# Four residual layers on one NeuronCore: where averages, halo copies, loads and banks stand in the issue order

## The chip, the cores and the metric

The kernel runs on one core of a Trainium2 chip as a single launch. Its engines each work through their own instruction queue in order: TensorE (PE in the profile, its weight loads PEld), VectorE (DVE), ScalarE (ACT), GpSimd (POOL) and SyncE (SP, which only issues DMAs). The metric is the device time of the launch in microseconds. The kernel before was timed three times.

## What is computed

The input is 1024 images of 16 x 16 positions and 16 channels in float32. Four layers follow, each of the form x + layer(group norm of x). The norm takes the mean and variance of pairs of channels over an image.

```python
x = x + _L0_conv_ref(_gn(x), core0, core1, core2)     # tensor train
x = x + _L1_conv_ref(_gn(x), ...)                     # cellular automaton
x = x + _L2_conv_ref(_gn(x), filters, bias)           # 3x3 convolution
x = x + _L3_conv_ref(_gn(x), ...)                     # as layer 1

# layers 1 and 3, per image:
p = jnp.concatenate([xt, y1, y2], axis=1)       # y1, y2: Sobel filters
flat = p.reshape(B * W * Hh, 48)
h = jax.nn.relu(flat @ fc0_w.T + fc0_b)         # first dense layer, 128 wide
d = (h @ fc1_w.T + fc1_b).reshape(B, C, W, Hh)  # second dense layer
mask = (pre & post)                             # 3x3 maxima of channel 3
```

Layer 0 is a matrix of 4096 x 4096 in tensor-train form, with ranks 16, applied to each image.

## The kernel before

The batch is cut into two chunks of 512 images, and a chunk fills one of two resident tiles of 32 lines (`XN`, 128 partitions x 512 each line). A chunk is either in the layout "cw" (channels and columns chosen by the line) or "wc". Every engine's order is written out by hand: the program is run as Python, and instructions are issued in the order in which the functions are called (`tc.manual_schedule`). A float32 product leaves two matmul records in the profile; a transpose leaves one.

`run` (L1534) drives each stretch. It takes a list of main steps, the products of a layer, and background lists with costs in microseconds. Each background step gets a due point between 0 and 1 from the costs; bare numbers are pauses. After main step i all background steps that are due are issued, in order. At the last main step everything left is issued.

Layer 0 runs as five phases of 16 units. `build` (L1045) makes a unit's weights in four banks `pw` of the "w" pool from a tile `gq`, which SP loads from `g_dram` (L1040); ScalarE copies them out (L1062). During the first phase (main steps: 64) the background turns the rest of the first chunk by transposes `ptin` (L866), loads the second chunk in eight loads of 1 MB on POOL's queue (`load`, L848), makes further tiles g (`gs`, L581, stored by SP, L563) and turns the second chunk. These transposes and g products take banks by the tag "mw", which alternates between the pools "w" (four banks) and "m" (one bank) by the variable `either` (L144). POOL also stores the turned lines (L881).

Layers 1 and 3 (`layer_nca`, one run for each chunk: four "dense runs" in the text) go by `plan`: a slot is either a set of row tiles of 32 x 128 of the first dense layer (`ph`, L1521, evicted by ScalarE, L1524) or a block of the second dense layer (`po`, L1358, four column tiles of 128 x 32, evicted by VectorE, L1370). Some three to five row slots lie between two dense slots. `po` has two banks, tagged "o", and the averages of the background norm take theirs from the same two (`psum`, with `shared` set to "o").

The background norm of the other chunk is `norm_cw` (L782), by quarters of eight lines, or `norm_lines` (L709). Sums run on VectorE; a mean is a product with an averaging matrix (`pmean`, L749 or L717), the variance likewise (`pvar`, L753 with 32 columns, L721 with 128). ScalarE copies the mean (`held`), VectorE subtracts it; squares run on ScalarE in layer 2 and on VectorE in the dense runs.

Layer 2 (`layer_conv`, L1190) has 54 main steps for a chunk. Each row h has products of three row offsets (`inner`, L1222) in two banks and one contribution across halves (`across`, L1231) that reads a halo tile `hx`. ScalarE fills a halo tile in eight copies (L1210), queued in `pending`, one issued after each main step until the queue is empty. ScalarE also evicts the banks (`finish`, L1270), and POOL adds them to DRAM by DMA. Six banks hold three rows.

The last dense run turns its output for storing: `turn` (L1416) transposes into `ptx`, VectorE copies, and with the last tile SP stores 1 MB pieces to the output. The last four quads are done in two halves of the batch (`hf` 0 and 1), and `after(n, fn)` delays fn by n slots.

Of the kernel before, what the change touches and what calls it, by code (L numbers as in the profile page):

```python
# [19 lines left out]
P = 128  # L20
# [83 lines left out]
def conv_preact_kernel(ctx: ExitStack, tc: tile.TileContext, a: dict, out: bass.AP):  # L104
# [35 lines left out]
    either = [0]  # L140
# [567 lines left out]

    def norm_lines(X, on_act=True):  # L709
# [3 lines left out]
        st = {}  # L713

        def mean():
            st["p"] = psum([P, NB], "pmean")
            T.matmul(st["p"], gm_wc, s1["s"], start=True, stop=True)  # L717

        def var():
            st["v"] = psum([P, NB], "pvar")  # L720
            T.matmul(st["v"], gm_wc, s2["s"], start=True, stop=True)  # L721
# [5 lines left out]
        subs = each(X, 0, NL, lambda: st["m", 0], ALU.subtract)  # L727
        steps = steps + [5, mean, 2, held(st), 2] + centred(subs, more)
# [3 lines left out]
    def parts_cw(X, on_act):  # L732
# [3 lines left out]
        for q in range(4):  # L736
# [10 lines left out]
            def mean_q(s1=s1):  # L747
                st["p"] = psum([P, NB], "pmean")
                T.matmul(st["p"], gm_cw, s1["s"], start=True, stop=True)  # L749
# [17 lines left out]
            N["mean"].append(mean_q)  # L767
            N["var"].append(var_q)
# [13 lines left out]
    def norm_cw(X, on_act):  # L782
# [6 lines left out]
        for q in (1, 2):  # L789
            steps += woven(  # L790
                sums[q + 1], (1, var[q - 1]), (3, keep[q - 1]), (3, mean[q]), (4, hold[q])
            ) + [2] + sq[q][:4]
            if q == 1:
                steps += sq[q][4:]
# [231 lines left out]
    def layer_train():  # L1026
# [18 lines left out]
        def build(u):  # L1045
# [7 lines left out]
            pw = [bank([P, 2, 16 - 4 * k0, S], "w", "pw") for _ in range(4)]  # L1053
            for v in range(2):
# [135 lines left out]
    def layer_conv(X, n, other):  # L1190
# [64 lines left out]
        def step(*fs):  # L1255
            def go():
                for f in fs:
                    f()
                if pending:
                    pending.pop(0)()  # L1260

            return go
# [22 lines left out]
    def layer_nca(X, n, l, L, xo=None):  # L1285
# [119 lines left out]
        def residual(q, w2, hf=None):  # L1405
# [7 lines left out]
            else:  # L1413
                after(8, lambda: turn(q, w2, r, hf))
# [66 lines left out]
        def step(slot):  # L1481
            def go():
# [4 lines left out]
                else:  # L1487
                    for x in slot:
                        tile_of_row(*x)
                due = [fn for n, fn in later if n <= t]  # L1490
# [43 lines left out]
    def run(layer, us, loads, *spans, by=0.0):  # L1534
# [21 lines left out]
        for i, step in enumerate(main):  # L1556
# [5 lines left out]
            while todo and (todo[0][0] < part or i == len(main) - 1):  # L1562
                todo.pop(0)[1]()
# [23 lines left out]
    with ExitStack() as es:  # L1587
# [33 lines left out]
        ]  # L1621
        run(
            steps_of(phases[0]), 130, (),
            (late[:6] + loads[0:4] + late[6:] + loads[4:] + later + woven_in + tail + normed(0, 1) + combined(0, False), 0.0, 1.0),
# [35 lines left out]
    with ExitStack() as es:  # L1660
# [8 lines left out]
            (lambda: None, main1), 108, load_cw(X0, xf[3][0]) + [put(L3)], (norm_cw(X0, True), 0.09, 1.06), by=0.07  # L1669
# [38 lines left out]
```

## Time and profile before

| what | value |
|---|---|
| median of three runs | 3043.31 us (3041.16 to 3043.62) |
| the profiled execution: its time / its span | 3039.35 us / 3037.6 us |
| mean granted TensorE clock | 0.992 |
| layer 0, first phase and what lies ahead of it | 0 to about 192 us |
| layer 0, other phases | about 192 to 1759 us |
| layer 1, two dense runs | about 1760 to 2276 us |
| layer 2, two chunks | about 2277 to 2494 us |
| layer 3, two dense runs | about 2494 to 3020 us |
| last stores | to 3037.6 us |

TensorE is busy 98% of the span, but a busy TensorE isn't one at its peak: the ends of matmuls are modelled, and at half clock it is busy too. So the profile is read by the start times of successive operations in the timeline: 56 records of 128 x 512 of an undisturbed unit take 24.23 us. A bracket behind a line of the timeline gives the idle time before it and the engine whose work ended it.

### The profile page before, as it was taken

The page shows a single profiled execution, that of the slowest core. Times are in us where ns is not written, and L with a number is a line of the kernel's source. Part 1 is how long each engine was busy: PE and PEld are TensorE (multiplying, and loading weights), DVE is VectorE, ACT ScalarE, POOL GpSimd, SP SyncE. Part 2 cuts the span into 40 slices and gives each one's busy share as a digit, 9 for nine tenths or more (in the row PEclk, how much of TensorE's full clock was granted, in tenths as well). Part 3 has the DMA queues.
Part 4 walks back from the last instruction along what each step waited for, and adds up shares of the span by engine and source line. Part 5 has one row for each costly group of instructions (what it writes and reads, how often), then busy time and mean ns, then how long its engine had stood idle before and what let it go on. Part 6 is the DMA issues. An engine that isn't in the chain of part 4 may idle for free.

```text
span 3037.6 us, 36802 instructions
## 1 busy us (share of the span) xinstructions
PE 2973.1 (98%) x13810; PEld 1245.4 (41%) x13810; DVE 1764.0 (58%) x2352; ACT 1102.7 (36%) x1822; POOL 669.9 (22%) x727
## 2 busy tenths in 40 slices
PE   7999999999999999999999999999999999999997
PEld 4444334444444444444444433333333333333333
DVE  5354337555554555544555668756977765856433
ACT  4431441000000000000101156666667656666564
POOL 2135670200000000000000015434542223442321
PEclk9999999999999999999999999999999999999998
DMA  8643664533334333332222235436337866343466
GB/s 313 232 120 99 150 152 145 166 109 109 109 109 158 115 109 109 109 102 89 88 89 94 71 130 168 137 119 204 124 122 182 188 97 207 126 129 111 134 176 208
DMA packets 251522, 418.39 MB, mean 138 GB/s; under 512 B 34869, under 2 KB 105065, under 8 KB 248273
## 3 DMA queue, kind: packets, MB, share of 16 engines
q1 hardware_dynamic: 225776, 362.53, 36.2%
q0 software_dynamic: 25376, 53.38, 8.5%
q8 instruction: 109, 1.79, 0.2%
q14 instruction: 69, 0.56, 0.1%
q10 hardware_dynamic: 192, 0.13, 0.0%
HBM read 238.58 MB, written 165.53 MB: 133 GB/s over the span
## 4 chain that ended last, share of the span: by engine, by line
PE 92%; DVE 2%; DMA 1%; issue 1%; ACT 1%; POOL 1%; SPq 0%; DVEq 0%; POOLq 0%; ACTq 0%
PE po L1134 51%; PE ph L1521 22%; PE po L1358 8%; PE po L1222 4%; PE pw L1057 3%; PE po L1231 1%; PE L_conv_pe L392 1%; PE ptin L866 1%; DVE bn L860 1%; PE ptx L1420 1%; PE pvar L753 1%; PE pr L765 0%; PE pmean L749 0%; POOL res L1410 0%; ACT hx L1210 0%
## 5 line engine op out<-in xcount | busy, mean ns | idle before, releaser
L1134 PE MATMUL po<-xn,w 128*128 128x512 f32 x3584 | 1573.9, 596 | 1.2 <-DVE xn L946 1.1
L1134 PEld LDWEIGHTS po<-xn,w 128*128 128x128 f32 x3584 | 670.3, 190 | 839.8 <-issue 820.6
L1524 ACT ACTIVATE hid<-ph,pack 128x512 f32<-128x512 f32 (+1 forms) x1040 | 656.2, 680 | 381.3 <-PE ph L1521 267.7
L1170 DVE TENSOR_TENSOR r<-r,po 128x512 f32<-128x512 f32 x576 | 377.9, 684 | 577.4 <-PE po L1134 525.0
L1409 POOL TENSOR_TENSOR u<-u,mask 128x512 f32<-128x512 f32 x123 | 192.9, 1568 | 1815.3 <-DVE mask L1403 1395.6
L1062 ACT COPY w<-pw 128x512 f32<-128x512 f32 (+1 forms) x320 | 150.6, 556 | 1209.9 <-issue 1006.3
L1521 PE MATMUL ph<-xn,wq 32*128 32x512 f32 (+1 forms) x3752 | 568.8, 600 | 0.0
L1521 PEld LDWEIGHTS ph<-xn,wq 32*128 32x128 f32 x3752 | 239.4, 184 | 268.2 <-issue 235.9
L1521 PE MATMUL ph<-xn,pack 32*128 32x512 f32 x1288 | 298.6, 624 | 4.9 <-ACT hid L1524 3.0
L1358 PE MATMUL po<-hid,pack 128*32 128x512 f32 (+1 forms) x2080 | 282.1, 602 | 0.0
L1075 DVE TENSOR_TENSOR w<-w 128x512 f32<-128x512 f32 x320 | 210.9, 686 | 88.7 <-ACT w L1062 88.6
L655 DVE TENSOR_TENSOR xn<-xn,m 128x1024 f32<-128x1024 f32 x160 | 216.0, 1380 | 47.2 <-ACT m L678 47.0
L1410 POOL TENSOR_TENSOR res<-res,u 128x512 f32<-128x512 f32 x123 | 205.4, 1670 | 9.7
L1370 DVE SCALAR_TENSOR_TENSOR u<-po,pack,xn 128x512 f32<-128x512 f32 (+1 forms) x130 | 96.3, 741 | 189.9 <-PE po L1358 185.6
L1222 PE MATMUL po<-xn,convw 128*128 128x512 f32 x368 | 167.8, 608 | 2.9 <-ACT conv L1270 2.9
L1521 PEld LDWEIGHTS ph<-xn,pack 32*128 32x128 f32 x1288 | 115.1, 185 | 104.1 <-issue 64.6
L1170 DVE TENSOR_TENSOR xn<-xn,po 128x512 f32<-128x512 f32 x96 | 64.4, 684 | 123.7 <-PE po L1134 123.3
L1358 PEld LDWEIGHTS po<-hid,pack 128*32 128x32 f32 x2080 | 43.6, 108 | 193.0 <-issue 142.3
L622 DVE TENSOR_TENSOR sq<-sq 128x1024 f32<-128x1024 f32 x78 | 109.8, 1408 | 13.3 <-ACT sq L640 12.6
L1222 PEld LDWEIGHTS po<-xn,convw 128*128 128x128 f32 x368 | 69.1, 192 | 100.3 <-issue 91.5
L404 POOL DMA_DIRECT2D L_conv_wy<-xn x160 | 89.1, 565 | 27.5 <-ACT xn L398 16.2
L1057 PE MATMUL pw<-R,gq 32*128 32x256 f32 (+1 forms) x1280 | 88.4, 381 | 3.1 <-DMA gq<-g_dram 2.9
(166 smaller groups left out, 1770.1 us busy)
## 6 DMA issues: line engine op xcount, KB each, us to landing
xf<-r SPq DMA_DIRECT2D x112, 512.0 KB, 3.8
xn<-xf SPq DMA_DIRECT2D x96, 512.0 KB, 5.1
r<-xf SPq DMA_DIRECT2D x80, 512.0 KB, 4.5
wq<-L_conv_wy SPq DMA_DIRECT2D x192, 192.0 KB, 2.7
res<-xf SPq DMA_DIRECT2D x128, 256.0 KB, 3.2
xf<-res SPq DMA_DIRECT2D x96, 256.0 KB, 2.1
res<-xr SPq DMA_DIRECT2D x256, 64.0 KB, 2.8
xf<-conv POOLq DMA_DIRECT2D x64, 256.0 KB, 5.9
```

The costliest lines, as they stand in the source:

```text
L655: V.tensor_tensor(part, part, m().unsqueeze(1).broadcast_to([P, 2, NB]), op)
L1057: T.matmul(pw[r][:, v], st["g", u][rows, v], st["R"][rows, p % 2, 64 * k0 : 256], start=True, stop=True,)
L1062: A.copy(w[:, k0:4, :, 32 * r : 32 * r + 32].rearrange("p k t (v o) -> p v (k t) o", v=2), pw[r],)
L1075: V.tensor_tensor(w[:, k], w[:, x], w[:, y], ALU.add if sign > 0 else ALU.subtract)
L1134: T.matmul(po, st["w", u][:, matrix, t], x, start=t == 0, stop=t == 3)
L1170: V.tensor_tensor(r[at], r[at], po, ALU.add if sign > 0 else ALU.subtract)
L1222: T.matmul(st["po", h][wh], conv["fw"][:, y], X[:, 16 * wh + h + y - 1], start=y == max(0, 1 - h), stop=y == min(2, S - h),)
L1358: T.matmul(po[32 * j : 32 * j + 32], nca["w1"][:, v], hid[j], start=v == 0, stop=v == 1)
L1409: by.tensor_tensor(u, u, st["m"][:, w2, cols(hf)], ALU.mult)
L1410: by.tensor_tensor(r, r, u, ALU.add)
L1521: T.matmul(ph, w, x, start=k == 0, stop=k == len(tiles) - 1)
L1524: A.activation(h, ph, AF.Relu, bias=nca["bt"][:, r : r + 1])
```

## The change

There are seven edits. `average` makes the product with the averaging matrix: as one product where the shared pool is "m", as four column tiles of 32 where it is "o". `beside_dense` marks the means and variances; `run` holds a marked step, and all background steps behind it, until the main step just issued was a block of the second dense layer or the last one. A main step without the attribute `dense` (layers 0 and 2) counts as near. In `norm_cw` the variance of the quarter before stands one sum later. `build` sets `either`, so that the next "mw" bank comes from the pool "m". The halo copies of layer 2 are issued after four of every seven main steps (numbers 2, 4, 6 and 7), not after each. The turn in the last halves is due after four slots, not eight. The eight loads of the second chunk are put between the turns, and between the products of g, one for every two of these. In layer 2 the second chunk's background norm begins at 0.12 of the stretch, not 0.09.

```diff
@@ -706,6 +706,19 @@
 
         return [2, root, 3, (6, newton)]
 
+    def beside_dense(fn):
+
+        fn.beside = True
+        return fn
+
+    def average(out, w, x):
+        if shared[0] == "m":
+            T.matmul(out, w, x, start=True, stop=True)
+            return
+
+        for c in range(0, P, 32):
+            T.matmul(out[c : c + 32], w[:, c : c + 32], x, start=True, stop=True)
+
     def norm_lines(X, on_act=True):
         parts = [lambda l=l: X[:, l : l + 2] for l in range(0, NL, 2)]
         s1, steps = line_sum(parts, "s1", False)
@@ -714,17 +727,18 @@
 
         def mean():
             st["p"] = psum([P, NB], "pmean")
-            T.matmul(st["p"], gm_wc, s1["s"], start=True, stop=True)
+            average(st["p"], gm_wc, s1["s"])
 
         def var():
             st["v"] = psum([P, NB], "pvar")
-            T.matmul(st["v"], gm_wc, s2["s"], start=True, stop=True)
+            average(st["v"], gm_wc, s2["s"])
 
         def keep():
             st["ve"] = work([P, NB], "n", "ve")
             V.tensor_scalar(st["ve"], st["v"], GN_EPS, None, ALU.add)
 
         subs = each(X, 0, NL, lambda: st["m", 0], ALU.subtract)
+        mean, var = beside_dense(mean), beside_dense(var)
         steps = steps + [5, mean, 2, held(st), 2] + centred(subs, more)
         steps += [5, var, 2, keep] + rstd(st)
         return steps + by_rows(each(X, 0, NL, lambda: st["r"], ALU.mult))
@@ -746,7 +760,7 @@
 
             def mean_q(s1=s1):
                 st["p"] = psum([P, NB], "pmean")
-                T.matmul(st["p"], gm_cw, s1["s"], start=True, stop=True)
+                average(st["p"], gm_cw, s1["s"])
 
             def var_q(rows=rows, s2=s2):
                 st["v"] = psum([P, NB], "pvar")
@@ -764,8 +778,8 @@
                 st["p"] = psum([P, NB], "pr")
                 T.matmul(st["p"], sel[rows], st["r"][rows], start=True, stop=True)
 
-            N["mean"].append(mean_q)
-            N["var"].append(var_q)
+            N["mean"].append(beside_dense(mean_q))
+            N["var"].append(beside_dense(var_q))
             N["keep"].append(keep_q)
             N["held"].append(held(st, q))
             N["spread"].append(spread_q)
@@ -788,7 +802,7 @@
         steps = sums[0] + woven(sums[1], (2, mean[0]), (3, hold[0])) + [1] + sq[0]
         for q in (1, 2):
             steps += woven(
-                sums[q + 1], (1, var[q - 1]), (3, keep[q - 1]), (3, mean[q]), (4, hold[q])
+                sums[q + 1], (2, var[q - 1]), (3, keep[q - 1]), (3, mean[q]), (4, hold[q])
             ) + [2] + sq[q][:4]
             if q == 1:
                 steps += sq[q][4:]
@@ -1051,6 +1065,8 @@
 
             k0 = 2 if m1 == 2 else 0
             pw = [bank([P, 2, 16 - 4 * k0, S], "w", "pw") for _ in range(4)]
+
+            either[0] = 1
             for v in range(2):
                 for r in range(4):
                     rows = slice(32 * r, 32 * r + 32)
@@ -1256,7 +1272,9 @@
             def go():
                 for f in fs:
                     f()
-                if pending:
+
+                st["n"] = st.get("n", 0) + 1
+                if pending and st["n"] % 7 % 2 == 0:
                     pending.pop(0)()
 
             return go
@@ -1411,7 +1429,7 @@
             if xo is None:
                 after(7, lambda: nc.sync.dma_start(tile_cw(xf[l + 1][n], 8 * q + w2), r))
             else:
-                after(8, lambda: turn(q, w2, r, hf))
+                after(8 if hf is None else 4, lambda: turn(q, w2, r, hf))
 
         def turn(q, w2, r, hf):
             g0, n = (0, 4) if hf is None else (2 * hf, 2)
@@ -1487,6 +1505,7 @@
                 else:
                     for x in slot:
                         tile_of_row(*x)
+                go.dense = isinstance(slot, int)
                 due = [fn for n, fn in later if n <= t]
                 later[:] = [x for x in later if x[0] > t]
                 for fn in due:
@@ -1560,6 +1579,9 @@
                 loads[done]()
                 done += 1
             while todo and (todo[0][0] < part or i == len(main) - 1):
+                near = getattr(step, "dense", True) or i == len(main) - 1
+                if getattr(todo[0][1], "beside", False) and not near:
+                    break
                 todo.pop(0)[1]()
 
     def put(L):
@@ -1619,9 +1641,15 @@
         woven_in = [
             x for j in range(2) for i in range(4) for x in stat[j][i] + lines[j][4 * i : 4 * i + 4]
         ]
+
+        def mixed_in(xs, ys):
+
+            n = len(xs)
+            return [z for i, x in enumerate(xs) for z in (*ys[2 * i : 2 * i + 2], x)] + ys[2 * n :]
+
         run(
             steps_of(phases[0]), 130, (),
-            (late[:6] + loads[0:4] + late[6:] + loads[4:] + later + woven_in + tail + normed(0, 1) + combined(0, False), 0.0, 1.0),
+            (late[:6] + mixed_in(loads[0:4], late[6:]) + mixed_in(loads[4:], later) + woven_in + tail + normed(0, 1) + combined(0, False), 0.0, 1.0),
         )
         run(
             steps_of(phases[1]), 350, (),
@@ -1666,7 +1694,7 @@
         bg = bg[:-16] + woven(bg[-16:], *[(6 + i, copy) for i, copy in enumerate(first1)])
         run((lambda: now(first0), main0), 108, load_wc(X1, xf[2][1]), (bg, 0.09, 1.04), by=0.07)
         run(
-            (lambda: None, main1), 108, load_cw(X0, xf[3][0]) + [put(L3)], (norm_cw(X0, True), 0.09, 1.06), by=0.07
+            (lambda: None, main1), 108, load_cw(X0, xf[3][0]) + [put(L3)], (norm_cw(X0, True), 0.12, 1.06), by=0.07
         )
     with ExitStack() as es:
         shared[0] = "o"
```

## The prediction

> **What bounds the kernel now.** I read the page first (busy shares, slices, chain of waits), then TensorE's timeline in each stretch the diff touches, then ScalarE, VectorE and the DMA windows there.
>
> ```profile
> PE 2973.1 (98%) x13810; PEld 1245.4 (41%) x13810; DVE 1764.0 (58%) x2352; ACT 1102.7 (36%) x1822; POOL 669.9 (22%) x727
> PE 92%; DVE 2%; DMA 1%; issue 1%; ACT 1%; POOL 1%; SPq 0%; DVEq 0%; POOLq 0%; ACTq 0%
> ```
>
> TensorE carries the chain. From 480 to 1759 us a unit of 56 product records takes 24.23 us with nothing between but its build, and the diff doesn't touch that. What can be won is where TensorE waits, switches its tiling, or runs at a lower clock. TensorE's timeline, layer 0, first phase (start, length, operation, idle before it and its releaser):
>
> ```profile
> 61.91 0.48 PE L1057 MATMUL pw<-R,gq 32*128 32x128 f32 x2
> 63.03 0.48 PE L1057 MATMUL pw<-R,gq 32*128 32x128 f32 x2 [0.65 <-DMA gq<-g_dram]
> 66.24 1.19 PE L1057 MATMUL pw<-R,gq 32*128 32x128 f32 x10 [0.88 <-DMA gq<-g_dram]
> 67.36 1.97 PE L866 MATMUL ptin<-ident,xn 128*128 128x128 f32 x8
> 69.12 3.62 PE L1134 MATMUL po<-xn,w 128*128 128x512 f32 x4
> 72.54 1.09 PE L866 MATMUL ptin<-ident,xn 128*128 128x128 f32 x8
> ...
> 104.39 0.73 PE L1057 MATMUL pw<-R,gq 32*128 32x128 f32 x16
> 105.56 1.09 PE L866 MATMUL ptin<-ident,xn 128*128 128x128 f32 x8 [0.44 <-ACT w L1062]
> ...
> 114.77 0.73 PE L1057 MATMUL pw<-R,gq 32*128 32x128 f32 x16
> 115.43 1.17 PE L866 MATMUL ptin<-ident,xn 128*128 128x128 f32 x8
> ```
>
> The build at 61.91 waits for gq, whose DMA takes 13.22 us in the chain against a median of 2.2: the four 1 MB input loads were issued at 50.37. Then four records take 3.42 us (69.12 to 72.54) where they otherwise take 1.72: half clock. At 104.39 the transposes follow the build after 1.17 us, at 114.77 after 0.66: the former's bank waits for the build's first ScalarE copy.
>
> The convolution (layer 2), TensorE and ScalarE:
>
> ```profile
> 2335.71 7.13 PE L1222 MATMUL po<-xn,convw 128*128 128x512 f32 x16
> 2345.78 5.40 PE L1222 MATMUL po<-xn,convw 128*128 128x512 f32 x8 [2.94 <-ACT conv L1270]
> ...
> 2398.63 1.13 PE L749 MATMUL pmean<-s1s,gm_cw 128*128 128x512 f32 x2 [2.39 <-DVE s1s L630]
> ...
> 2413.05 1.04 PE L753 MATMUL pvar<-s2s,gv_cw 128*32 128x512 f32 x2 [2.67 <-DVE s2s L630]
> 2414.03 3.67 PE L1222 MATMUL po<-xn,convw 128*128 128x512 f32 x4
> ...
> 2345.04 1.27 ACT L1270 ACTIVATE conv<-po,b 128x512 f32<-128x512 f32 x2
> ```
>
> Three stalls, 8.0 us. After the first, eight records take 5.33 us (3.44 at full clock, 1.9 lost); after the third, four take 3.47 (1.75 lost). The second lowers no clock.
>
> The dense layers (layers 1, 3), and the DMA windows at the very end (from the left: stretch, length, five engines, granted clock, DMA share, GB/s):
>
> ```profile
> 1844.67 1.12 PE L749 MATMUL pmean<-s1s,gm_cw 128*128 128x512 f32 x2
> 1845.73 0.70 PE L1521 MATMUL ph<-xn,wq 32*128 32x512 f32 x2
> ...
> 3013.00:3015.00 2.00, 2.00 (x24) 1.11 (x18) 0.38 (x2) 1.17 (x4) 0.00 (x0) 1.00 0.00 0
> 3020.00:3023.00 3.00, 0.00 (x0) 0.00 (x0) 0.50 (x2) 0.00 (x0) 0.00 (x0) 0.79 0.97 404
> ```
>
> A mean takes 1.06 us among row tiles, for 0.86 us of work. At the end the DMAs are idle until the first half's stores start at 3015.27, then move some 420 GB/s to the end: there the stores are the bound.
>
> **What the Trainium skill says.** "TensorE: Matmul & The Clock Gate", What's actually happening: the clock halves after an idle window of about 3.4 us that runs freely. Agrees in kind: 2.67 and 2.94 us of idleness halved it, 2.39 didn't. "TensorEngine Tiling (Array Packing)", Key Properties: changing the tiling mode drains the array; the 0.2 us above is that. "DMA: Bandwidth & Descriptors", Queues, rings and completion order: an engine alternates between rings by whole packets; it fits four small gq transfers taking 13 us beside four large loads. The first page (Architectural detail) calls ScalarE and VectorE strictly first-in first-out; the late eviction at 2345.04, queued behind squares and copies, agrees.
>
> **The change part by part.** Against the profiled execution: span 3037.6 us, 3039.35 with what lies around it. The median of the runs shown, 3043.31, is 3.96 above; I carry the difference over to it.
>
> *Loads one by one.* Only one load, not four, then stands before the gq of 51.43, and the pairs of line stores lie between the loads on POOL. The stretch 61.91 to 72.54 is 10.63 us; at full pace it is 0.66 (build) + 0.87 (8 transposes) + 1.72 (4 records) = 3.25. Gain 7.4. What is late next: POOL waits for no product, and between the second four loads there is no POOL work (the g builds use TensorE, ScalarE, SP), so these four still go back to back, about 71 us in the new order. But two g builds now come right before them, so the 512 KB store of g goes onto SP ahead of m_dram and the gq that the build of unit 5 needs (about 76 issued, needed near 85.5; four loads at some 400 GB/s occupy the DMAs 10 us). Bounds 0 to 4 us; I take 1.3, about half of one to three. Net 6.1. Statistics and turns of the second chunk keep their places, 10 us or more after the loads land.
>
> *Other bank behind builds.* In nine of the builds (at 40.87, 92.39, 104.39, 124.71, 134.65, 144.59, 154.53, 164.46, 174.40) the next work takes a "w" bank and begins 1.17 instead of 0.66 us later: 9 x 0.51 = 4.6. The second turn then gets the "w" bank, 0.43 us later, when the copy is done, as at 115.43. One g pair now follows a build directly: minus 0.5. Net 4.1.
>
> *Averages beside the dense layer.* Eleven means (full array) become four column tiles like those of the second dense layer, and together with eight one-column variances (L753) wait until a dense step has run. A lone mean costs 1.06 plus about 0.2 for closing the row group before it; beside a dense block 0.86. By due times six lie alone (0.4 each), five already next to one (0.2): 3.4. Six of the variances lie alone (0.3 each): 1.8. Cost: an average that isn't let through holds all background work behind it, up to 4 us. VectorE has that slack (73% busy in the first dense run), and the delayed sums remove no cover. But with variance one step later, two pairs (variance of quarter 1 with mean of 2 in the first run; of 0 with mean of 1 in layer 3) fall due at one dense step. The second then needs one of only two "o" banks: it waits for an eviction of VectorE (0.69 us for the variance, behind an addition of 1.22), about 1 us; the first such wait stands there now too (0.97 at 2600.80). Net 5.2 - 1.5 = 3.7; bounds -3 (each wait doubled, some clock) to 7.
>
> *Even copies, layer 2.* The eviction that ends the first stall goes behind seven halo copies since its group began (1.04 us each); now four. But it also stands behind a square whose subtraction VectorE ends at 2342.72; VectorE loses 0.70 to a late square at 2335.82, and that goes. So square done 2343.1, one copy to 2344.15, eviction 0.85 us sooner: stall 2.94 to 2.1. Under the 2.39 that halved nothing, so 1.9 of clock comes back: 2.8. Bounds 0.5 (clock still drops) to 4.8.
>
> *Layer 2, second chunk.* Start 0.12: the first mean falls one step later (1.72 us), its stall 2.39 becomes 0.65. The first variance falls two steps later (3.44): TensorE comes at 2410.37 - 2.39 + 0.65 + 3.44 = 2412.1 for a sum at 2413.05, stall 1.0 instead of 2.67, and the clock (1.75) holds. Sum 5.2. VectorE's chain is the limit afterwards: it gains about 2.6 us from the earlier mean, TensorE 5, so an eviction behind squares is late next, about 1.2. Net 4.0; bounds 1 to 6.8.
>
> *Last halves.* The turn of the first half (ptx at 3014.15) moves four slots forward, to when its sum is ready (3011.93): 1.9 us, with 0.3 for short waits. The stores start that much sooner and fill the DMAs to the end, so the end moves by 1.9; bounds 1 to 2.6.
>
> Sum: 6.1 + 4.1 + 3.7 + 2.8 + 4.0 + 1.9 = 22.6 us. Profiled 3016.8; median 3043.3 - 22.6 = 3020.7.
>
> **The rivals.** (1) Everything clears: 7.4 + 4.6 + 6 + 4.8 + 6.8 + 2.2 = 31.8, 3011.5. For it: each stall has one named releaser. Against: in layer 2 VectorE's chain stands just behind. (2) New waits take the place: gq of unit 5 costs 4 with clock, layer 2 gives 2 in all, the averages nothing: 3.4 + 4.1 + 0 + 2 + 1.9 = 11.4, 3031.9. For it: in-order ScalarE behind VectorE-paced squares. (3) Nothing to measure: the averages lose 10 and layer 2 gives 1, total 0.4 us gained, 3043. For it: only that TensorE is busy 98%. (4) Slower: held averages release background work in bursts, evictions on VectorE come late, and TensorE waits in the dense runs long enough for the clock. The stall of 2.97 us at 1779.94, followed by half clock until about 1785, shows the price: 3 + 2.5 = 5.5 us. The other parts give 18.9, so from five such stalls among the 19 averages it is slower; eight give 44 - 18.9 = 25 lost, 3068. Against: the sum of the dense block's own output is issued to VectorE ahead of the burst.
>
> **How the numbers follow.** Forecast 0.46 (3015 to 3027), (1) 0.24, (2) 0.18, (3) 0.07, (4) 0.05. A measurement tells about 0.2% from no change, 6 us. The first three are faster: 0.88; same 0.07; slower 0.05. Range 3009 to 3033: it takes in (1) and (2) and leaves out (3), (4) and the outer ends.
>
> **What would show it.** Right: no wait for gq near 62 and full clock to 75; 0.66 us behind every build; the stall near 2345 under 2.4 us without half clock; first store of the last halves some 2 us sooner before the end. Wrong: a gq wait near unit 5; a mean waiting over 2 us for VectorE in a dense run; evictions of layer 2 later than now.

## The result

The changed kernel takes 3022.86 us (median of four runs, 3019.86 to 3025.54), the kernel before 3043.47 (four runs, 3041.16 to 3044.03): ratio 0.9933, 95% interval 0.9916 to 0.9951. The forecast was 3020.7. The profiled execution took 3019.86 us with a span of 3018.2, so 19.4 us of span went, against 22.6 in the sum. Line numbers of the changed kernel are some 14 to 22 higher (`po` of layer 0 L1150, `pw` L1073, `ph` L1540, `po` of the convolution L1238, its eviction L1288).

The page of the changed kernel, busy times and chain:

```profile
PE 2964.6 (98%) x13876; PEld 1244.8 (41%) x13876; DVE 1766.5 (59%) x2352; ACT 1103.9 (37%) x1822; POOL 671.4 (22%) x727
PE 91%; DVE 3%; DMA 2%; issue 1%; ACT 1%; POOL 1%; SPq 0%; DVEq 0%; ACTq 0%; POOLq 0%
```

TensorE still carries the chain, but DMA's share of it has grown from 1% to 2%: a first hint of where gain was given back. The chain's pieces there are `gq<-g_dram` of 10.23 and 12.27 us, for the builds of units 4 and 5.

The starts of the same event in the two timelines give the gain of each stage:

| stage | before, us | after, us | gained | predicted |
|---|---|---|---|---|
| first products to the build of unit 1 | 1.91 | 3.72 | -1.8 | 0 |
| build of unit 1 to the first build of phase 1 | 158.87 | 154.13 | 4.7 | loads 6.1 + banks 4.1 |
| phases 1 to 4 | 1560.83 | 1560.83 | 0.0 | 0 |
| three dense runs (layer 1 twice, layer 3's first) | 774.90 | 766.96 | 7.9 | 3.7 |
| layer 2, first chunk | 108.80 | 106.29 | 2.5 | 2.8 |
| layer 2, second chunk | 108.07 | 103.66 | 4.4 | 4.0 |
| last dense run to the end | 285.26 | 283.71 | 1.6 | 1.9 |

The sum came out near, but two terms are off in opposite directions. TensorE's timeline after, at the builds of units 3, 4 and 5 (start, length, operation, idle before it and its releaser):

```profile
63.64 0.73 PE L1073 MATMUL pw<-R,gq 32*128 32x128 f32 x16
64.29 1.17 PE L880 MATMUL ptin<-ident,xn 128*128 128x128 f32 x8
...
74.02 0.48 PE L1073 MATMUL pw<-R,gq 32*128 32x128 f32 x2
75.09 0.48 PE L1073 MATMUL pw<-R,gq 32*128 32x128 f32 x2 [0.59 <-DMA gq<-g_dram]
75.94 0.46 PE L1073 MATMUL pw<-R,gq 32*128 32x128 f32 x2 [0.36 <-DMA gq<-g_dram]
76.80 0.56 PE L1073 MATMUL pw<-R,gq 32*128 32x128 f32 x9 [0.41 <-DMA gq<-g_dram]
...
80.02 3.78 PE L1150 MATMUL po<-xn,w 128*128 128x512 f32 x4
...
94.01 1.47 PE L1073 MATMUL pw<-R,gq 32*128 32x128 f32 x16 [1.05 <-DMA gq<-g_dram]
```

Unit 3's build no longer waits: 0.66 us, then transposes at full clock. That is the 7.4 us foretold. But unit 4's build now waits three times, the four product records at 80.02 run at half clock, and unit 5's build waits again. The stretch from 74.02 to 84.64 takes 10.6 us, against about 5.1 at full pace; unit 5 costs about 1.8 more. So 7.3 came back. POOL's timeline shows why:

```profile
54.30 0.57 POOL L862 DMA_DIRECT2D xn<-in_x_dram  x1
59.35 0.57 POOL L862 DMA_DIRECT2D xn<-in_x_dram  x1
63.66 0.57 POOL L862 DMA_DIRECT2D xn<-in_x_dram  x1
67.56 0.57 POOL L862 DMA_DIRECT2D xn<-in_x_dram  x1
...
74.58 1.65 POOL L862 DMA_DIRECT2D xn<-in_x_dram  x3
76.65 0.53 POOL L862 DMA_DIRECT2D xn<-in_x_dram  x1 [0.42 <-DMA xr<-lines]
```

The first four loads are some 4 us apart, since stores of turned lines stand between them, and each store waits for ScalarE; the second four go back to back. From 65 to 95 us the DMAs are 98 to 101% busy.

TensorE's timeline in layer 2, after:

```profile
2338.04 3.70 PE L1238 MATMUL po<-xn,convw 128*128 128x512 f32 x8 [2.12 <-ACT conv L1288]
...
2388.36 1.10 PE L716 MATMUL pmean<-s1s,gm_cw 128*128 128x512 f32 x2
...
2403.60 1.05 PE L767 MATMUL pvar<-s2s,gv_cw 128*32 128x512 f32 x2 [1.08 <-DVE s2s L630]
```

The first stall is 2.12 us (2.94 before) and its eight records take 3.70, full clock. The mean waits for nothing (2.39 before), the variance 1.08 (2.67). The DMA windows of the end (stretch, length, busy times of PE, PEld, DVE, ACT and POOL, clock, DMA share, GB/s):

```profile
2994.00:2996.00 2.00, 2.00 (x30) 1.29 (x27) 0.74 (x3) 1.49 (x4) 0.00 (x0) 1.00 0.04 8
2998.00:3001.00 3.00, 2.19 (x22) 0.77 (x20) 2.00 (x6) 0.90 (x3) 0.00 (x0) 1.00 0.97 399
```

The first store goes out at 2995.80, 22.4 us before the end, as before (3015.27, 22.4): the stores fill the DMAs to the end and the end moves with their start.

### The profile page after: what moved, and what is told of

The parts are those of the page before. It is cut to its first block, busy times and chain, and to the rows that moved or that the text cites. A ratio compares the mean times of both kernels' runs of the same rounds, so it can differ in the third digit from the quotient of the medians.

```text
span 3018.2 us, 36937 instructions
## 1 busy us (share of the span) xinstructions
PE 2964.6 (98%) x13876; PEld 1244.8 (41%) x13876; DVE 1766.5 (59%) x2352; ACT 1103.9 (37%) x1822; POOL 671.4 (22%) x727
## 4 chain that ended last, share of the span: by engine, by line
PE 91%; DVE 3%; DMA 2%; issue 1%; ACT 1%; POOL 1%; SPq 0%; DVEq 0%; ACTq 0%; POOLq 0%
PE po L1150 51%; PE ph L1540 22%; PE po L1376 8%; PE po L1238 3%; PE pw L1073 3%; PE L_conv_pe L392 1%; DMA gq<-g_dram 1%; PE ptin L880 1%; PE po L1247 1%; DVE sq L622 1%; PE ptx L1438 1%; DVE xn L655 1%; PE pr L779 0%; DMA xn<-in_x_dram 0%; POOL res L1428 0%
## 5 line engine op out<-in xcount | busy, mean ns | idle before, releaser
L1150 PE MATMUL po<-xn,w 128*128 128x512 f32 x3584 | 1575.7, 596 | 0.7 <-DVE xn L960 0.7
L1150 PEld LDWEIGHTS po<-xn,w 128*128 128x128 f32 x3584 | 670.6, 190 | 839.2 <-issue 820.6
L1078 ACT COPY w<-pw 128x512 f32<-128x512 f32 (+1 forms) x320 | 150.6, 557 | 1211.0 <-issue 1006.3
L1540 PE MATMUL ph<-xn,wq 32*128 32x512 f32 (+1 forms) x3752 | 565.0, 599 | 0.0
L1540 PEld LDWEIGHTS ph<-xn,wq 32*128 32x128 f32 x3752 | 240.2, 184 | 263.8 <-issue 232.7
L1540 PE MATMUL ph<-xn,pack 32*128 32x512 f32 x1288 | 296.7, 623 | 4.9 <-ACT hid L1543 3.0
L655 DVE TENSOR_TENSOR xn<-xn,m 128x1024 f32<-128x1024 f32 x160 | 216.9, 1386 | 37.7 <-ACT m L678 37.5
L1238 PE MATMUL po<-xn,convw 128*128 128x512 f32 x368 | 164.0, 598 | 3.2 <-ACT conv L1288 3.2
L1540 PEld LDWEIGHTS ph<-xn,pack 32*128 32x128 f32 x1288 | 114.2, 185 | 104.3 <-issue 64.8
L1238 PEld LDWEIGHTS po<-xn,convw 128*128 128x128 f32 x368 | 68.2, 190 | 98.5 <-issue 88.4
L1073 PE MATMUL pw<-R,gq 32*128 32x256 f32 (+1 forms) x1280 | 89.6, 383 | 2.4 <-DMA gq<-g_dram 2.4
```

The costliest lines, as they stand in the source:

```text
L655: V.tensor_tensor(part, part, m().unsqueeze(1).broadcast_to([P, 2, NB]), op)
L1073: T.matmul(pw[r][:, v], st["g", u][rows, v], st["R"][rows, p % 2, 64 * k0 : 256], start=True, stop=True,)
L1078: A.copy(w[:, k0:4, :, 32 * r : 32 * r + 32].rearrange("p k t (v o) -> p v (k t) o", v=2), pw[r],)
L1150: T.matmul(po, st["w", u][:, matrix, t], x, start=t == 0, stop=t == 3)
L1238: T.matmul(st["po", h][wh], conv["fw"][:, y], X[:, 16 * wh + h + y - 1], start=y == max(0, 1 - h), stop=y == min(2, S - h),)
L1540: T.matmul(ph, w, x, start=k == 0, stop=k == len(tiles) - 1)
```

## Half clock by chance, and the equal-clock table

Before the experiments one thing has to be taken out of the numbers. Phases 1 to 4 are the same code in every kernel below, yet took 1560.8, 1562.5 or 1564.2 us. The timeline and the windows (columns as above) of the changed kernel near 326 us:

```profile
326.25 1.54 PE L392 MATMUL L_conv_pe<-xn 9*36 9x512 f32 x8 [0.70 <-ACT w L1078]
327.72 1.98 PE L1150 MATMUL po<-xn,w 128*128 128x512 f32 x4
```

```profile
330.00:335.00 5.00, 5.00 (x18) 2.01 (x11) 1.32 (x3) 2.71 (x5) 3.26 (x7) 1.00 0.62 201
```

and of the run with plain averages (below), same instructions, same wait:

```profile
325.99 1.54 PE L392 MATMUL L_conv_pe<-xn 9*36 9x512 f32 x8 [0.70 <-ACT w L1078]
327.46 2.86 PE L1150 MATMUL po<-xn,w 128*128 128x512 f32 x4
```

```profile
330.00:335.00 5.00, 5.00 (x13) 1.54 (x13) 0.69 (x1) 2.71 (x5) 2.94 (x7) 0.50 0.47 167
```

In the second the clock is halved from 328.4 to 335.3 us behind the same 0.70 us wait, and 3.4 us are lost. "TensorE: Matmul & The Clock Gate" of the Trainium skill (What's actually happening) has the idle window, of about 3.4 us, run freely; that fits a halving that comes or not with the phase of the window.

The traces show such a window. In each of the fourteen profiles all changes of the granted clock lie whole multiples of 3.413 us apart, to within 0.006 us over the whole span, and each stretch of half clock, apart from the one at the end, lasts one to four such windows, each costing 1.7 us. But idleness need not fill a window, as the page has it. In layer 2 there are eighteen waits of TensorE of more than 2 us. Where the largest part of the wait in a single window was 2.03 us or more, half clock followed (seven cases); where it was 1.87 or less, it did not (eleven). So the wait of 2.39 us before, cut into 1.52 and 0.87 by the edge of a window, lowered no clock, and a wait of 2.11 us that fell into one window did (plain averages, below).

In phase 0 (the first phase), from the build of unit 1 on, idleness alone doesn't decide: of the windows at full clock, half clock followed one with 0.41 us of it and didn't follow one with 1.60. Counted together with the time in which only weight builds or products of g ran (32 and 16 rows), it decides again: the clock halved after all fourteen windows with 2.36 us or more, and after none with 2.24 or less. So these small products count there much like idleness. The same count doesn't separate all cases in phases 1 to 4 (halved at 2.45, not halved at 3.01), so their exact weight stays open.

Since the windows lie differently in each execution, part of every stage's time is chance. So beside raw stage times I give times "at equal clock": from each stage (1 - granted clock) times length is taken off, over windows of about 4 us (8 in phases 1 to 4) whose clock is under 0.985. Checked on phases 1 to 4, this leaves 1560.7 to 1560.8 in all kernels. Elsewhere it doesn't take out all chance. Seven kernels, the changed one among them, have the same code in phase 0: they took 152.6 to 155.1 us there raw and 147.5 to 151.7 at equal clock. Seven have the same code in the three dense runs: 767.0 to 770.2 raw, 761.7 to 763.8 at equal clock. A difference between two profiles that is smaller than this scatter isn't shown by them.

| us, at equal clock (raw) | phase 0 from the build of unit 1 | three dense runs | layer 2 |
|---|---|---|---|
| before | 155.5 (158.9) | 768.1 (774.9) | 213.5 (216.9) |
| after | 150.4 (154.1) | 763.6 (767.0) | 210.0 (210.0) |
| old loads | 150.8 (154.5) | 761.7 (770.2) | 210.9 (210.9) |
| banks only | 151.3 (154.7) | 767.1 (773.9) | 212.0 (213.6) |
| plain averages | 151.7 (155.1) | 768.1 (773.3) | 209.9 (211.6) |
| split only | 151.3 (154.7) | 765.7 (772.5) | 209.2 (210.9) |
| hold only | 150.6 (154.1) | 764.2 (771.0) | 210.7 (210.7) |

## Experiments: loads and banks

The diffs show only the part of a line that differs. In them `late` holds the turns of the first chunk that are left, `later` the products of g, `woven_in` the statistics and turns of the second chunk.

Old order of loads in the changed kernel:

```diff
-late[:6] + mixed_in(loads[0:4], late[6:]) + mixed_in(loads[4:], later) + woven_in
+late[:6] + loads[0:4] + late[6:] + loads[4:] + later + woven_in
```

> The changed kernel, with the second chunk's loads issued four together again, as before. My theory (the moved loads won 7.4 us at the build of unit 3 and gave about 7.3 back at the builds of units 4 and 5): the total stays within 2 us of the changed kernel's, 3021 to 3025; in the trace the wait for gq and the half clock are at unit 3 again, units 4 and 5 have none, and the first build of phase 1 starts at 196 to 198 us, against 196.75. Rival A (the waits at units 4 and 5 come from the banks: with each build 0.5 us shorter TensorE runs ahead of its gq): the waits at units 4 and 5 stay and unit 3's comes back, 7 us longer, 3030. Rival B (the loads gave the 6.1 us that were predicted, the start of the run took it): 6 us longer, 3029, with no wait at 4 and 5.

3025.99 us (ratio to before 0.9945, 0.9931 to 0.9959). Phase 0 takes 154.54 us against 154.13; unit 3 waits 0.84, 1.29 and 0.95 us for gq, then half clock; units 4 and 5 wait for nothing. My theory holds for the stage; the 0.4 us lies inside its scatter. The span is 7.0 us longer; phase 0 gives 0.4 of it, phases 1 to 4 and the three dense runs, which the edit doesn't touch, 4.9, with one window of half clock more in each of the four. That took the total past my 3021 to 3025.

One line of the change alone, in the kernel before:

```diff
 pw = [bank([P, 2, 16 - 4 * k0, S], "w", "pw") for _ in range(4)]
+either[0] = 1
```

> The kernel before with one line of the change: the other bank behind each build. My theory (a term of 4.1 us: nine builds at 0.51 each, with 0.5 given back): from the build of unit 1 to the first build of phase 1 it takes 154 to 155.5 us, against 158.9 before, every build of phase 0 is followed after 0.66 us, the waits for gq at unit 3 stay (longer by up to 1 us, since TensorE comes sooner), total 3037 to 3040. Rival (what a build saves is waited for at the next gq): 157.5 us or more, total 3042.

3034.40 us (0.9981, 0.9973 to 0.9989); phase 0 takes 154.70 us, 4.2 less than before. As expected, with unit 3's waits longer (0.56, 1.28, 0.93 us). The total is 5.5 us under before, more than I said; in its profile layer 2's second chunk, where its code is that of before, took 105.06 us, not 108.07: the first mean waited 1.02 us, not 2.39, and no half clock followed the variance's wait of 2.73. Neither comes from the edit. From both sides, then: banks 4.2, loads 0.4 to 0.6; with the scatter of phase 0 (152.6 to 155.1 us where the loads are the changed kernel's, against 154.5 and 154.7 here) the loads gave between nothing and some 2 us.

The second four loads later:

```diff
-late[:6] + mixed_in(loads[0:4], late[6:]) + mixed_in(loads[4:], later) + woven_in
+late[:6] + mixed_in(loads[0:4], late[6:]) + later + woven_in
...
-for x in stat[j][i] + lines[j][4 * i : 4 * i + 4]
+for x in [loads[4 + i]] * (j == 0) + stat[j][i] + lines[j][4 * i : 4 * i + 4]
```

> The changed kernel, with the second four loads moved behind the g builds, one ahead of each quarter of the first half's statistics. My theory (the four loads issued back to back at 74.6 us hold the small gq transfers of units 4 and 5): both waits shrink to under 0.4 us, no half clock after them, phase 0 ends 5 to 7 us sooner (first build of phase 1 at 190 to 192), total 3016 to 3018. Rival A (the first four loads and the line stores fill the DMAs by themselves): the wait at unit 4 stays with its half clock, only unit 5's goes, 1 to 2 us, total 3021. Rival B (the late loads make the second half's statistics or turns wait): a new wait of TensorE for transposes between 110 and 160 us, total not better than 3023.

3020.91 us (0.9936, 0.9924 to 0.9949). Unit 5's wait is gone, unit 4's stays (0.26, 0.36 and 0.42 us) with half clock after it; first build of phase 1 at 193.31. That is rival A, in the place of the wait and in the total: the first four loads and the line stores fill the DMAs by themselves.

The same with three turns ahead of each of the first four loads:

```diff
-(*ys[2 * i : 2 * i + 2], x)] + ys[2 * n :]
+(*ys[3 * i : 3 * i + 3], x)] + ys[3 * n :]
```

> As the run with the second four loads moved behind the g builds, and the first four with three turns ahead of each, not two. My theory: if unit 4 still waits with the first four as they are, it no longer does here, 3016 to 3018; if it didn't wait, this changes nothing (within 1 us in the trace up to the first build of phase 1). Rival (the loads are needed soon): the second chunk's first turns wait for the last of the first four loads, 2 us or more later.

3017.41 us (0.9922, 0.9910 to 0.9935), the fastest measured; its interval overlaps the changed kernel's, but the profile places the gain: phase 0 takes 148.71 us, 5.4 less than the changed kernel's and 3.9 less than the shortest of the seven kernels with its phase 0. TensorE's timeline:

```profile
73.54 0.73 PE L1073 MATMUL pw<-R,gq 32*128 32x128 f32 x16
74.09 1.33 PE L554 MATMUL pg<-cores,xn 16*128 16x128 f32 x8
75.82 0.72 PE L554 MATMUL pg<-cores,xn 16*128 16x128 f32 x8 [0.40 <-ACT g L557]
76.47 3.68 PE L1150 MATMUL po<-xn,w 128*128 128x512 f32 x4
```

No build waits for gq any more, as expected for a wait that the first four loads cause. Yet four records take 3.61 us, half clock, after 0.40 us of idleness; the products with 32 and 16 rows ahead of them take 2.9 us, that wait included, and all of it lies in one window. Two runs tried to win that too. In the first, the g builds stand among the turns of the first half:

```diff
-late[:6] + mixed_in(loads[0:4], late[6:]) + later + woven_in
+late[:6] + mixed_in(loads[0:4], late[6:]) + woven_in
...
-for x in [loads[4 + i]] * (j == 0) + stat[j][i] + lines[j][4 * i : 4 * i + 4]
+for x in ([loads[4 + i]] + stat[0][i] + [later[2 * i]] + lines[0][4 * i : 4 * i + 2]
+          + [later[2 * i + 1]] + lines[0][4 * i + 2 : 4 * i + 4] if j == 0
+          else stat[j][i] + lines[j][4 * i : 4 * i + 4])
```

> As the run with all loads wide apart, with the eight g builds no longer in one block but two beside each quarter of the first half's turns, a load ahead of each quarter. In that run TensorE was at half clock from 76.5 us with only 0.4 us of idleness before it, after 2.9 us of a build and two g builds, which use 32 and 16 rows of the array; and four g builds waited 0.49 us each for ScalarE's copy. My theory (small products count as idleness for the clock; copies hide once g builds are apart): no half clock between 60 and 120 us, no wait for ACT g above 0.2, phase 0 from the first build 145 to 147 us (148.7 in that run), total 3015. Rival (g builds displace turns, TensorE then waits for the second half's transposes or for banks): 148.5 or more.

3018.09 us (0.9926, 0.9913 to 0.9940), phase 0 152.2 us: the rival's side. The first turn came so early that it waited for the last of the first four loads, 2.47 us, with half clock after it, and the copy's wait of 0.45 to 0.49 us stayed. In the second, the g builds stand apart, ahead of these turns, and the variance comes one step later only in the convolution:

```diff
-late[:6] + mixed_in(loads[0:4], late[6:]) + later + woven_in
+late[:6] + mixed_in(loads[0:4], late[6:]) + woven_in
...
+][4 * 5 :]
+woven_in = [
+    x for i in range(4) for x in [later[2 * i], loads[4 + i], later[2 * i + 1]] + stat[0][i]
+] + lines[0] + woven_in
...
-(2, var[q - 1]), (3, keep[q - 1])
+(1 + on_act, var[q - 1]), (3, keep[q - 1])
```

> As the run with all loads wide apart, with the eight g builds set apart by the second four loads and the first half's statistics, ahead of the first half's turns (when the g builds stood among the turns, the first turn waited 2.5 us for the last of the first four loads), and the variance one step later only in the convolution. My theory: no wait for gq, none for loads, none of 0.49 us for ScalarE's copy, from the build of unit 1 to the first build of phase 1 145 to 147 us (148.7 with all loads wide apart, of which 1.7 are half clock), dense runs 0.5 us shorter than the changed kernel's at equal clock, total 3014 to 3016. Rival (a g build costs its 0.65 us and the copy's wait wherever it stands, and half clock comes by chance): 147.5 or more, total 3017 to 3018.

3027.61 us (0.9950, 0.9936 to 0.9963): wrong, and it shows the mechanism best. POOL's timeline, then TensorE's:

```profile
74.35 2.24 POOL L862 DMA_DIRECT2D xn<-in_x_dram  x4
77.01 0.53 POOL L862 DMA_DIRECT2D xn<-in_x_dram  x1 [0.43 <-DVE w L1091]
```

```profile
90.09 0.79 PE L1073 MATMUL pw<-R,gq 32*128 32x128 f32 x2 [5.16 <-DMA gq<-g_dram]
91.86 0.79 PE L1073 MATMUL pw<-R,gq 32*128 32x128 f32 x2 [0.98 <-DMA gq<-g_dram]
93.47 0.76 PE L1073 MATMUL pw<-R,gq 32*128 32x128 f32 x2 [0.82 <-DMA gq<-g_dram]
```

I had put g builds and statistics between the loads, and neither has any work on POOL. POOL waits for none of them (the 0.43 us in the bracket stand before the last load of such a group in other profiles too, behind another engine each time), so five loads went out within 3.2 us, and gq of unit 5 took 13.36 us in the chain. Distance in the program is no distance in time on a queue that has nothing to wait for. In the faster run the second four loads stood among turns, whose stores do hold POOL: they were issued at 74, 103.9, 113.3 and 122.8 us. Here the g builds were apart: the window with the build of unit 4 and the first of them held 1.8 us of small products, and what followed ran at full clock until the wait. The dense runs, expected to be 0.5 us shorter than the changed kernel's at equal clock, took 764.1, 0.5 longer.

## Experiments: averages

Plain averages: one product, let through at once.

```diff
-if shared[0] == "m":
+if True:
-fn.beside = True
+fn.beside = False
```

> The changed kernel, with every average as one product on the full array and let through at once, as before (the variance one step later is kept). In the traces the three dense runs gained 7.9 us against 3.7 predicted. My theory (the switch of tiling costs more than the 0.2 us I took, both for means and for variances; 1.4 us of the second run's gain is a stretch of half clock that only the profile of the kernel before had): the three runs together are 5 to 7 us longer than in the changed kernel, total 3028 to 3030. Rival (the dense runs gained by the later variance and by chance in the clock, the averages themselves gave 3.7 or less): 2 to 3.7 us longer in the three runs, total 3025 to 3026.5.

3030.33 us (0.9962, 0.9949 to 0.9974); the dense runs take 773.3 us, 6.3 more, within what I expected. But at equal clock they take 768.1 against 763.6 (before: 768.1): the averages are worth 4.5 us between these two profiles (4.3 to 6.4 against the seven kernels with the same dense runs), and 3.4 of the 7.9 us won there were two half-clock stretches that the profile before had, in layer 1's second run and layer 3's first, and the one after had not. The prediction's 3.7 was somewhat low; my reading of 7.9 as work was wrong.

Each half of the edit by itself, the first with only the second of these two lines, the second with only the first:

> The changed kernel with the averages in four column tiles, but let through at once, wherever they fall due. The three dense runs took 767.0 us in the changed kernel, 773.3 with plain averages, 774.9 before. My theory (what saves is that the average lies beside a dense block of the same tiling, so that one switch goes): split alone gives at most a quarter, 771.5 to 773.5 us in the three runs, total 3028. Rival (a full-array product is itself the dear thing, it fills and drains all four row groups): split alone gives most of it, 767 to 769, total 3023 to 3025.

> The changed kernel with every average held until a dense step has run, but as one product on the full array. My theory (place decides): 768 to 770 us in the three dense runs, most of the 6.3 us, total 3024 to 3026. Rival (split decides): 771.5 us or more, total 3028.

Split alone: 3026.05 us (0.9951, 0.9940 to 0.9963), dense runs 772.5 raw, 765.7 at equal clock. Hold alone: 3024.45 us (0.9947, 0.9935 to 0.9959), 771.0 raw, 764.2 at equal clock. The raw figures bear out the first expectation and neither theory of the second. At equal clock place gives 3.9 of the 4.5 us and the split 2.4. The difference between the two is inside the scatter of the three runs together, but the second and third run, where the same code takes 498.4 to 499.2 us at equal clock in seven kernels, show the order: plain averages 502.6, split alone 501.7, hold alone 500.0. Place does most of it. That the two don't add up because both save the same switch is argued, not shown.

## Experiments: layer 2 and the end

A halo copy after every step:

```diff
-if pending and st["n"] % 7 % 2 == 0:
+if pending:
```

> The changed kernel with a halo copy after every convolution step, not after even ones. The first chunk's convolution took 106.3 us in the changed kernel (108.8 before), the second's 103.7 (108.1 before). My theory: the stall after the first step group is 2.9 us again and the clock halves after it, first chunk 2.5 us longer, second chunk within 0.7, total 3025.5. Rival A (the first stall is set by the square that VectorE delays, and the clock came by chance): the stall stays near 2.1, first chunk within 0.7 us, total as the changed kernel. Rival B (the copies stand before evictions and squares everywhere): both chunks longer, 4 us or more together.

3022.92 us (0.9941, 0.9928 to 0.9953); a run to run spread of 11 us hides the effect in the time, the trace doesn't:

```profile
2338.49 5.40 PE L1238 MATMUL po<-xn,convw 128*128 128x512 f32 x8 [2.93 <-ACT conv L1288]
```

The stall and the half clock are back to what they were, the first chunk takes 108.80 us, 2.5 more, as before to the hundredth; the second is 0.2 longer. My theory holds in the trace, with a reservation on the clock. A first stall of 2.11 to 2.38 us stood in eleven profiles of kernels with even copies, and half clock followed in two of them (plain averages, split only), those in which all of it fell into one window; stalls of 2.67 to 2.94 us stood six times in layer 2 and half clock followed five times, the sixth being cut into 1.44 and 1.28 us. A shorter stall makes half clock rarer, it doesn't rule it out. An estimate from these figures: if some 2.0 us in one window of 3.41 are needed, a stall of 2.11 us that falls anywhere halves the clock in about 45% of the cases, one of 2.93 in about 70%. Then the shorter stall saves on average 0.8 us of waiting and only about 0.4 of the 1.7 us of clock.

The variance one step earlier:

```diff
-(2, var[q - 1]), (3, keep[q - 1])
+(1, var[q - 1]), (3, keep[q - 1])
```

> The changed kernel with the variance one step earlier again, as before; the start at 0.12 is kept. The run with the start at 0.09 cost the second chunk's convolution nothing: the mean waited 1.14 us and the variance not at all. My theory (the later variance is what won in that stage: TensorE has 1.7 us more work before it): the variance waits 2.5 to 2.8 us, the clock halves after it, the stage is 2.5 to 3.5 us longer, 106.2 to 107.2, and the first and last dense runs are each up to 1 us shorter, since no two averages fall due at one dense step; total 3024.5. Rival (VectorE's chain from the landing of the loads sets that stage, wherever the averages stand): within 0.7 us of 103.7.

3027.53 us (0.9958, 0.9945 to 0.9970). TensorE's timeline:

```profile
2402.90 1.04 PE L767 MATMUL pvar<-s2s,gv_cw 128*32 128x512 f32 x2 [2.80 <-DVE s2s L630]
2403.88 3.41 PE L1238 MATMUL po<-xn,convw 128*128 128x512 f32 x4
```

The variance waits 2.80 us and half clock follows; the second chunk takes 107.99 us, 4.3 more, above what I expected: 1.7 of wait, 1.7 of clock, and 0.9 besides. The second variance stands apart among full-array products there, where in the changed kernel it runs among `across` products of its own 32-column tiling. The changed kernel's lines, then this run's:

```profile
2418.30 0.62 PE L767 MATMUL pvar<-s2s,gv_cw 128*32 128x512 f32 x1 [0.26 <-DVE s2s L630]
2418.31 0.62 PE L1247 MATMUL po<-hx,convw 128*32 128x512 f32 x2
...
2419.07 1.05 PE L767 MATMUL pvar<-s2s,gv_cw 128*32 128x512 f32 x2
2420.04 1.98 PE L1238 MATMUL po<-xn,convw 128*128 128x512 f32 x4
```

That place costs 1.2 us (the variance and its eight `across` products take 1.85 us together there, 3.0 here with what the switch adds to the full-array products), and a later wait gives 0.3 back; that the tiling is the cause is argued. In both kernels the first variance begins 27.5 us after the start of the stage: VectorE's sum sets it, and a later place only puts more work ahead of it. The dense runs take 763.0 us at equal clock against 763.6, inside the scatter: not shown to be shorter.

The start at 0.09 again, and the last halves turned after 8 slots:

```diff
-(norm_cw(X0, True), 0.12, 1.06)
+(norm_cw(X0, True), 0.09, 1.06)
-after(8 if hf is None else 4, lambda: turn(q, w2, r, hf))
+after(8, lambda: turn(q, w2, r, hf))
```

> The changed kernel with the second chunk's norm beside the convolution starting at 0.09 again and the last halves turned after 8 slots again; the variance one step later is kept. The two edits act in different stages. Theory for the first: the wait of the first mean is 2.4 us again, but it brings TensorE later to the variance, whose wait stays near 1 us with no half clock, so the second chunk's convolution is 1.7 us longer, 105.4 us. Rival: the variance waits 2.7 us again and the clock halves, 4.4 us longer, 108.1. For the second: the last dense run is 1.5 us longer (285.2 against 283.7); rival (the stores are bound by the DMAs' total, not by their start): within 0.4. Total by my theories 3026.

3023.87 us (0.9950, 0.9938 to 0.9963). The second chunk:

```profile
2388.95 1.12 PE L716 MATMUL pmean<-s1s,gm_cw 128*128 128x512 f32 x2 [1.14 <-DVE s1s L630]
...
2403.76 1.05 PE L767 MATMUL pvar<-s2s,gv_cw 128*32 128x512 f32 x2
```

The mean waits 1.14 us, the variance not at all, and the stage takes 103.80 us against 103.66: neither expectation. What the mean waits here, the variance no longer waits; the first sum of VectorE's chain waits for the reloaded lines, in the kernel before 9.92 us:

```profile
2392.98 1.23 DVE L614 TENSOR_TENSOR s<-xn 128x1024 f32<-128x1024 f32 x1 [9.92 <-DMA xn<-xf]
```

So the start at 0.12 is worth 0.1, which can't be told from nothing, since nine kernels with the changed kernel's code in this stage took 102.9 to 104.4. The last dense run takes 285.36 us, 1.65 more, as expected.

## Why the prediction was right in sum, and where it failed

- **Loads (6.1): the failed term, measured at 0.4 to 0.6, some 2 at most.** The 7.4 us at unit 3 were right. What was mis-sized is "bounds 0 to 4 us; I take 1.3" for what is late next. The prediction saw that the second four loads would go back to back at about 71 us and named unit 5. It overlooked unit 4, whose four gq transfers are issued from 62.65 to 66.98, around loads 3 and 4, and land from 73.42 to 76.67: the first four loads, set apart by 4 us each and with line stores between them, still fill the DMAs, and unit 4's wait fell beside the small g products, with half clock after it. In the changed kernel's profile it cost 5.5, unit 5 1.8.
- **Banks (4.1): right, 4.2,** by the run with that line alone.
- **Averages (3.7): 4.5 of work** (4.3 to 6.4 with the scatter), at least 0.6 above my sum, and 3.4 by chance of the clock. The sum had 19 averages; the timelines have 20, the one-column variances being nine. The wait of two averages at one dense step came once (0.78 us in layer 1's first run); the 0.97 us wait in layer 3 went.
- **Even copies (2.8): 2.5, right in the stall, lucky in the clock.** The stall fell to 2.12 (2.1 foretold), worth 0.8; the other 1.7 is half clock, which after such a stall came in two of eleven profiles, not never. The prediction reasoned that 2.1 lies under the 2.39 that halved nothing; but that wait halved nothing because the edge of a window cut it.
- **Second chunk (4.0): 4.4, right in sum, wrong in one cause.** The prediction let both shifts add, 1.72 us each. The runs give 4.3 to the later variance (of which 1.2 is the second variance's place, which no term had) and 0.1 to the later start, because VectorE's chain begins when the reloaded lines land. That was in the trace: before its first sum there VectorE stood idle for 9.92 us, released by a DMA. How late they land varies: with the code of before, the mean waited 2.39 us in one profile and 1.02 in another, so part of the 4.4 may be chance, 1.4 of it in this wait, and so is whether 1.7 of clock goes with the variance's wait; the stage took 108.07 us in the one profile and 105.06 in the other. What the start at 0.12 is worth when the lines land late wasn't tried.
- **Last halves (1.9): 1.6,** and the first store keeps its 22.4 us to the end.
- **Chance in the clock,** which no term had: -1.8 at the start of layer 0, +3.4 in the dense runs.

Term by term: 22.6 - 5.5 (loads and banks) + 4.2 (averages) - 0.3 (copies) + 0.4 (second chunk) - 0.3 (last halves) - 1.8 (start) gives 19.3, against 19.4 measured. That the total came near is luck: the loads missed by 5.5 us, and the averages made up 4.2 of it, 3.4 of these by chance of the clock. Without chance in the clock the averages end at 4.5 and the start at 0, and the sum is 17.7: the forecast was nearer than its terms.

## What to carry to other kernels

A queue that waits for nothing issues at once, however far apart its instructions stand in the program: to space transfers, put each behind something that its own queue waits for, and look at every small transfer that is issued in that stretch, not only at the next one. A wait that is pushed back at one step shows up at the next if the chain that feeds both starts from something else; find that start before adding shifts. Where the clock halves by chance, compare stages at equal clock, and with the scatter of stages whose code is the same, before calling a difference work.

## What the runs showed of the hardware

The clock halved or not behind the same instructions and waits: in phases 1 to 4 it lost 0, 1.7 or 3.4 us; at the very start the first four records took 1.98 us in some runs and 3.48 to 3.78 in others. Its changes lay whole multiples of 3.413 us apart in each profile. In layer 2 what decided was the idleness inside one such window: half clock followed 2.03 us or more in all seven cases and 1.87 or less in none, so waits of 2.1 to 2.4 us halved the clock twice in twelve and waits of 2.7 to 2.9 us five times in six. In phase 0 products of 16 and 32 rows counted much like idleness. A gq transfer of 32 KB took 2.2 us at the median before, and 10 to 13 us in the chain beside 1 MB loads.
